# Second-layer attention: the first pass in blocks of 64 queries by 192 keys on quarters and halves of TensorE, and the next group's k and q fetched block by block

## Chip, core and metric

The kernel runs on one core of a Trainium2 chip. The metric is device time in microseconds (us), the median of some runs. Engines are named as in the profile: PE (TensorE, matrix multiply; PEld its weight loads), DVE (VectorE), ACT (ScalarE), POOL (GpSimd) and SP (SyncE, which issues most DMAs). DVE and ACT read PE's results from PSUM, which has eight banks of 512 float32 values in each of 128 partitions.

## The reference

Two layers follow each other on `x` of shape 2 x 2048 x 256. Each computes `xn = layernorm(x)`, a self-attention `s` of `xn`, a gate `g = silu(ffn(xn))`, and `x + s * g`. The change touches the second layer's attention, which is local:

```
qkv = x @ w_qkv + b_qkv          # 16 heads of 16 values
mask = 0 where |query - key| <= 64, else -inf
scores = q @ k.T * 0.25 + mask
attn = softmax(scores)
out = (attn @ v) @ w_out + b_out
```

So a query sees at most 129 keys, those up to 64 places before and after it. Everything is float32. The first layer's attention sees all keys, and uses the same functions with `local` false.

## The kernel before

**Layout.** `attention()` works by items: batch `b` (2), group `g` of four heads (4), and block `n` of 512 queries (4), 32 items in all. Of an item, q and k of the four heads lie in the four quarters of 32 partitions (`hp[j]`): 16 values of a head, then a row that holds minus the maximum in q and ones in k, so that the product `k.T q` comes out with the maximum already taken off. `qs` and `ks` hold two groups each, of all 2048 positions; k has 64 zeros (`PAD`) at either end. `fetch` (L581) reads the group after the next from DRAM (`qd`) into the tile of the group that is done, in two halves of 1024 positions, one after the group's second block and one after its fourth: four DMAs a group, on SP.

**A step.** In the second layer an item has two steps (`U = 2`), each of 256 queries, and 64 steps make the loop. `scores` (L596) issues two things side by side for a step:

- the second pass (`sk`, L611): scores with keys in partitions and queries along the row, for the step's 256 queries. Per head a bank of 512 columns, from three matmuls of 256, 128 and 128 columns. ACT takes the exponential out of PSUM (L683), POOL sets what lies outside the band to zero (L688).
- the first pass (`sq`, L653), five steps ahead (`LEAD + U`): scores with queries in partitions. Per head and tile of 128 queries one matmul against 256 keys (at the sequence's ends 192, by `reach`), in which the band lies. DVE adds a mask and takes the row's maximum in one instruction (`seen`, L674).

The four heads are in different partitions of q and k, so their matmuls use different quarters of PE's rows. When both passes are issued together (`apart`), the second pass of heads 0 and 1 stands beside the first pass of heads 2 and 3, and then the other way round. The list of matmuls is sorted by a number `when` that is written by hand: how far into the step a matmul belongs, in units of one matmul of 256 columns.

Two steps later `weigh` (L733) sums the values with the exponentials as weights (`acc`, L747): per head 128, 256 and 128 columns, the four heads in four groups of 32 columns of PE. ACT copies the result (`av`, L752).

**Maxima.** Once an item (so every second step), three steps ahead of its second pass, `place_max` (L714) turns the maxima with PE (`pmx`, L720); ACT changes the sign (`row`, L723) and issues the DMA that writes them into q (L726).

**After an item** a chain of DMAs on SP divides by the sums: `away` (L773, `ad`), `compact` (L782 and L783), `write` (L789), `spread` (L796, `recb`) and `divide` (L802, on POOL and DVE in turn). After the last group of a batch, `project` (L835, `pr`) multiplies by the output weights, and the result goes to `x` and out.

**Buffers.** PSUM's banks: `pmax` has two tiles of two banks, for `sq`; `pexp` has four of one bank, which sk, acc, pmx and pr take in turn. When an instruction of PE waits for a buffer, all later ones of PE wait with it.

The order on each engine is that of the program, settled when the program is built by a planner that knows the tiles' uses; instructions under `pin` keep their place.

Of the kernel before, what the change touches and what calls it, by code (L numbers as in the profile page):

```python
# [10 lines left out]
F32 = mybir.dt.float32  # L11
I32 = mybir.dt.int32
AF = mybir.ActivationFunctionType
ALU = mybir.AluOpType
# [3 lines left out]
P = 128  # L18
# [4 lines left out]
NG = 4  # L23
HP = 32
HV = HD + 1
TB = 512
# [11 lines left out]
def two_layers(ctx: ExitStack, tc: tile.TileContext, a, out):  # L38
# [445 lines left out]
    def attention(A, scale, local, final, start=None, projected=False):  # L484
# [18 lines left out]
        with ExitStack() as st:  # L503
# [43 lines left out]

            mp, op = pool("mp", 2), pool("op", 1)
            hp = [slice(j * HP, (j + 1) * HP) for j in range(NG)]
            ep = None if local else pool("ep", 8)  # L550


            pmax, pm = pool("pmax", 2, space=PSUM), pool("pexp", 4, space=PSUM)
            if local:

                mask = mp.tile([P, 2 * P], F32, name="mask", bufs=1)
                nc.vector.memset(mask, 0.0)
                nc.gpsimd.affine_select(
                    out=mask, in_=mask, compare_op=ALU.is_ge, fill=MASKED, base=0,
                    pattern=[[1, 2 * P]], channel_multiplier=-1,  # L560
                )
                nc.gpsimd.affine_select(
                    out=mask, in_=mask, compare_op=ALU.is_ge, fill=MASKED, base=P,
                    pattern=[[-1, 2 * P]], channel_multiplier=1,
                )

                efirst = xn[1].rearrange("p c t -> p (c t)").rearrange("p (i s c f) -> p i s c f", i=4, c=2, f=P)
                elast = op.tile([P, 2, 4, 2, P], F32, name="elast")
                ecount = [0]

                def exponentials():

                    r = ecount[0] % 6
                    ecount[0] += 1
                    return efirst[:, r] if r < 4 else elast[:, r - 4]
# [2 lines left out]
                b, g, n = items[i]  # L578
                return qs[(b * NG + g) % 2], ks[(b * NG + g) % 2], vs[b]

            def fetch(bg, lo=0, hi=T):  # L581

                if bg >= B * NG:
                    return
                b, g = divmod(bg, NG)
                k0, k1 = max(lo - PAD, 0), (T if hi == T else hi - PAD)
                for i, t in ((1, qs[bg % 2]), (0, ks[bg % 2])):
                    to, s = (slice(lo, hi), slice(lo, hi)) if i else (slice(PAD + k0, PAD + k1), slice(k0, k1))
                    nc.sync.dma_start(out=t[:, to], in_=qd[i, b, bass.ts(g, NG), :, s].rearrange("h w t -> (h w) t"))

# [5 lines left out]
            def scores(second, first, es):  # L596
# [7 lines left out]
                if second:  # L604
                    i, u = second
                    b, g, n = items[i]
                    q, k, _ = tiles(i)
                    if local:

                        qt = n * TT + 2 * u  # L610
                        segs = [  # L611
                            (P, 3 * P, bass.ts(qt + 1, P), bass.ds(qt * P, 2 * P)),
                            (0, P, bass.ts(qt, P), bass.ts(qt, P)),
                            (3 * P, 4 * P, bass.ts(qt + 2, P), bass.ts(qt + 1, P)),
                        ]
                    else:
                        segs = [(0, TB, bass.ts(u, P), bass.ts(n, TB))]
                    if local:
                        slots = [exponentials() for _ in range(2)]
                        for j in range(NG):  # L620
                            es[j] = slots[j // 2][:, 2 * (j % 2) : 2 * (j % 2) + 2].rearrange("p s c f -> p (s c f)")
                    else:
                        for j in range(NG):
                            es[j] = ep.tile([P, TB], F32, name="e", tag="e")
                    spare = None
                    for j in range(NG):
                        if not apart and j >= 2:
                            if spare is None:
                                spare = pmax.tile([P, 2, TB], F32, name="sk2", tag="sq")
                            t = spare[:, j - 2]  # L630
                        else:
                            t = pm.tile([P, TB], F32, name="sk", tag="m")
                        when = 2 * (j // 2) if apart else 0
                        for lo, hi, ks_, qs_ in segs:
                            pieces.append((when, t[:, lo:hi], k[hp[j], ks_], q[hp[j], qs_]))
                            when += 2 * (hi - lo) / TB
                        tasks.append((es[j], t))
                pairs = []
                if first:
                    i1, u1 = first  # L640
                    b1, g1, n1 = items[i1]
                    q1, k1, _ = tiles(i1)
                    if i1 not in part:
                        part[i1] = (
                            mp.tile([P, NG, TT], F32, name="mx", tag="mx"),
                            None if local else mp.tile([P, NG, TT, NB], F32, name="part", tag="part"),
                        )
                    mx, pt = part[i1]
                    for pair in ((2, 3), (0, 1)):
                        sq = pmax.tile([P, 2, TB], F32, name="sq", tag="sq")  # L650
                        pairs.append((pair, sq))
                        for d, j in enumerate(pair):
                            when = (2, 2, 0, 0)[j] if apart else 0  # L653
                            if local:
                                for t in range(2):
                                    qt, lo, hi = reach(n1, u1, t)
                                    pieces.append((
                                        when + t, sq[:, d, t * 2 * P + lo : t * 2 * P + hi],
                                        q1[hp[j], bass.ts(qt, P)], k1[hp[j], qt * P + lo : qt * P + hi],
                                    ))  # L660
                            else:
                                t, kb = divmod(u1, NB)
                                pieces.append((
                                    when, sq[:, d], q1[hp[j], bass.ds(n1 * TB + t * P, P)], k1[hp[j], bass.ts(kb, TB)]
                                ))
                for _, o, lhs, rhs in sorted(pieces, key=lambda x_: x_[0]):
                    nc.tensor.matmul(o, lhs, rhs, start=True, stop=True)  # L667
                for pair, sq in pairs:
                    if local:
                        for d, j in enumerate(pair):  # L670
                            for t in range(2):
                                qt, lo, hi = reach(n1, u1, t)
                                seen = mp.tile([P, 2 * P], F32, name="seen", tag="seen")
                                nc.vector.tensor_tensor_reduce(  # L674
                                    seen[:, lo:hi], sq[:, d, t * 2 * P + lo : t * 2 * P + hi], mask[:, lo:hi],
                                    1.0, LOWEST, ALU.add, ALU.max, mx[:, j, 2 * u1 + t : 2 * u1 + t + 1],
                                )
                    else:
                        nc.vector.tensor_reduce(pt[:, pair[0] : pair[1] + 1, t, kb], sq, AX.X, ALU.max)  # L679
# [4 lines left out]
                if second and local:  # L684
                    for e in slots[::-1]:

                        for c, sign in ((0, -1), (1, 1)):
# [1 line left out]
                                out=e[:, :, c, :], in_=e[:, :, c, :], compare_op=ALU.is_ge, fill=0.0, base=0,  # L689
                                pattern=[[0, 4], [sign, P]], channel_multiplier=-sign,  # L690
                            )

            def reach(n, u, t):

                qt = n * TT + 2 * u + t
                return qt, (PAD if qt == 0 else 0), (2 * P - PAD if qt == NT - 1 else 2 * P)

            pin = tc.keep_in_program_order

# [159 lines left out]
            for i, (b, g, n) in enumerate(items):  # L859
                if local:  # L860
                    at(i * U - LEAD, place_max, i)
                else:
                    at(i * U - LEAD, turn_max, i)
                    at(i * U - LEAD + 3, fetch_max, i)
                end = (i + 1) * U

                hops = (0, 1, 3, 4, 5, 7, 8) if local else (0, 2, 4, 5, 7, 11, 13)
                steps = (away, compact, invert, write, spread, divide)
                if i >= len(items) - (NB if local else 1):

                    hops, steps = (0, 1, 2), (last_there, last_back)
                    if not local:
                        continue
                for hop, f in zip(hops, steps):
                    at(end + DEL + hop, f, i)
                if g == NG - 1:
                    for oc in range(NC):
                        at(end + DEL + hops[-1] + oc, project, i, oc)
                if local and n == NB // 2 - 1:
                    at(end, fetch, b * NG + g + 2, 0, T // 2)  # L880
                if n == NB - 1:
                    at(end, fetch, b * NG + g + 2, T // 2 if local else 0)
            if start:
                at(0, start)
            if not local:
# [304 lines left out]
```

## Time and profile before

| what | us |
|---|---|
| median of three runs (2533.64 to 2539.33) | 2537.28 |
| the profiled execution | 2538.34 |
| its span, first to last instruction | 2536.6 |
| PE busy in it | 2513.1 |
| DVE busy | 1686.2 |
| ACT busy | 1620.8 |
| POOL busy | 876.6 |
| local attention: first first-pass matmuls | from 2248.2 |
| its first sum (acc) | 2298.8 |
| its last sum | 2519.3 |

The profile times every instruction of one execution. A row of groups gives line, engine, operation, shapes and count, then the busy time and the mean of one in ns, then the idle time before them and what ended it. A float32 matmul shows as two records, since PE makes two passes over its columns; records of different quarters overlap, so that PE's busy time isn't a measure of its work. A timeline gives start, length, engine, line and operation, with like neighbours merged. The chain lists what ended last, step by step back from the end; SPq and ACTq in it are DMAs being issued by these engines.

### The profile page before, as it was taken

To read this page: it belongs to the slowest core of one execution; us is meant where nothing else is said; L and a number is where in the kernel's file an instruction comes from. 1 tells how busy PE (TensorE), PEld (TensorE's weight loads), DVE (VectorE), ACT (ScalarE), POOL (GpSimd) and SP (SyncE) were. 2 spreads that over 40 slices of the span, in tenths; PEclk is the share of its full clock that TensorE was granted. 3 is DMA by queue.
4 is the path that set the end of the run, shared out by engine and by line. 5 is a ranking of instruction groups with operands and counts; after the bars stand their busy time and mean duration, and the time that the engine had idled before them with its cause. 6 is when DMAs were issued, how large, how long until landed. Compare 5 with 4: busy or idle time off the path is not lost.

```text
span 2536.6 us, 47898 instructions
## 1 busy us (share of the span) xinstructions
PE 2513.1 (99%) x18896; PEld 1060.6 (42%) x18896; DVE 1686.2 (66%) x2747; ACT 1620.8 (64%) x3187; POOL 876.6 (35%) x827
## 2 busy tenths in 40 slices
PE   8999999999999999999999999999999999999999
PEld 6444444444333333333333333333333334457766
DVE  4143333157888888888777788788888765238986
ACT  5400000126888888888888888888888886227755
POOL 0000000102444444444444444444444420016887
PEclk9999999999999999999999999999999999999999
DMA  6131111230001001001001001001000002133552
GB/s 243 50 84 51 52 51 39 82 118 14 14 14 43 16 12 44 16 12 44 16 12 43 10 18 44 12 17 43 15 14 10 14 14 63 49 133 108 163 167 81
DMA packets 146353, 129.83 MB, mean 51 GB/s; under 512 B 93456, under 2 KB 97936, under 8 KB 143568
## 3 DMA queue, kind: packets, MB, share of 16 engines
q1 hardware_dynamic: 144256, 125.46, 16.5%
q8 instruction: 148, 2.42, 0.4%
q10 hardware_dynamic: 1872, 1.31, 0.2%
q14 instruction: 77, 0.63, 0.1%
HBM read 80.50 MB, written 45.97 MB: 50 GB/s over the span
## 4 chain that ended last, share of the span: by engine, by line
PE 79%; DMA 1%; ACT 0%; POOL 0%; DVE 0%; issue 0%; ACTq 0%; SPq 0%; POOLq 0%; DVEq 0%
PE sk L667 25%; PE acc L747 22%; PE sq L667 19%; PE pp L477 5%; PE pr L835 2%; PE pp L532 2%; PE po L1027 1%; PE pt L1023 1%; PE po L1035 1%; PE xb L113 0%; PE xb L138 0%; DMA k<-qd 0%; PE of L827 0%; DMA q<-qd 0%; POOL xn L688 0%
## 5 line engine op out<-in xcount | busy, mean ns | idle before, releaser
L679 DVE TENSOR_REDUCE part<-sq 128x2 f32<-128x1024 f32 x1024 | 1207.3, 1221 | 294.3 <-PE sq L667 284.7
L683 ACT ACTIVATE e<-sk 128x512 f32<-128x512 f32 x2048 | 1058.3, 603 | 217.2 <-PE sq L667 197.7
L667 PE MATMUL sk<-q,k 32*128 32x512 f32 (+2 forms) x5632 | 1135.8, 533 | 1.2 <-ACT xn L683 1.0
L667 PE MATMUL sq<-k,q 32*128 32x512 f32 (+2 forms) x5120 | 1129.1, 569 | 0.5 <-DVE part L679 0.5
L761 POOL TENSOR_TENSOR av<-av,more 128x512 f32<-128x512 f32 x459 | 581.4, 1267 | 936.3 <-ACT more L760 931.1
L667 PEld LDWEIGHTS sk<-q,k 32*128 32x128 f32 x5632 | 522.0, 184 | 604.1 <-ACT e L683 512.5
L747 PE MATMUL acc<-e,v 128*32 128x512 f32 x4096 | 546.7, 605 | 0.0
L667 PEld LDWEIGHTS sq<-k,q 32*128 32x128 f32 x5120 | 402.3, 183 | 22.3 <-DVE part L679 13.2
L760 ACT COPY more<-acc 128x512 f32<-128x512 f32 x459 | 268.7, 585 | 1.2 <-PE acc L747 1.0
L747 PEld LDWEIGHTS acc<-e,v 128*32 128x32 f32 x4096 | 81.8, 108 | 388.2 <-ACT e L683 367.8
L461 ACT ACTIVATE gt<-po 128x512 f32<-128x512 f32 x16 | 8.8, 594 | 321.1 <-PE po L457 321.1
L674 DVE CUSTOM_DVE_ANT_0 seen<-sq,mask 128x256 f32<-128x256 f32 (+1 forms) x512 | 176.2, 410 | 53.6 <-PE sq L667 49.2
L467 POOL TENSOR_TENSOR x<-x,up 128x512 f32<-128x512 f32 x16 | 23.1, 1461 | 450.1 <-DVE up L464 277.5
L448 DVE TENSOR_TENSOR xs<-we,px 128x512 f32<-128x512 f32 x64 | 43.9, 686 | 136.2 <-PE px L440 130.3
L688 POOL TENSOR_SCALAR_AFFINE_SELECT xn<-xn 128x512 f32<-128x512 f32 x172 | 106.2, 652 | 77.4 <-ACT xn L683 75.7
L440 PE MATMUL px<-xn,FV 128*128 128x512 f32 x256 | 121.2, 595 | 0.0
L444 PE MATMUL py<-cum,FW 128*128 128x512 f32 x256 | 120.5, 593 | 0.6 <-DVE cum L412 0.6
L424 PE MATMUL po<-pr,UO 128*128 128x512 f32 x256 | 119.0, 592 | 0.0
L683 ACT ACTIVATE xn<-sk 128x512 f32<-128x512 f32 x172 | 89.8, 602 | 41.1 <-PE sk L667 17.9
L450 DVE TENSOR_TENSOR pr<-xs,py 128x512 f32<-128x512 f32 x64 | 44.0, 687 | 64.8 <-PE py L444 64.6
L424 PEld LDWEIGHTS po<-pr,UO 128*128 128x128 f32 x256 | 48.6, 190 | 61.2 <-issue 61.0
L444 PEld LDWEIGHTS py<-cum,FW 128*128 128x128 f32 x256 | 48.4, 190 | 61.5 <-issue 59.8
(195 smaller groups left out, 1604.0 us busy)
## 6 DMA issues: line engine op xcount, KB each, us to landing
we<-wd SPq DMA_DIRECT2D x128, 128.0 KB
ad<-av SPq DMA_DIRECT2D x59, 256.0 KB
qd<-sb SPq DMA_DIRECT2D x48, 256.0 KB
k<-qd SPq DMA_DIRECT2D x10, 1024.0 KB
q<-qd SPq DMA_DIRECT2D x10, 1024.0 KB
xn<-ad SPq DMA_DIRECT2D x59, 128.0 KB
recb<-rd SPq DMA_DIRECT2D x59, 128.0 KB
q<-qd SPq DMA_DIRECT2D x12, 512.0 KB
```

The lines of the kernel that those rows point to most:

```text
L424: nc.tensor.matmul(po[oc], UO[:, ch, bass.ts(oc, P)], pr, start=(ch == 0), stop=False)
L440: nc.tensor.matmul(px, FV[:, c, bass.ts(ch, P)], xn[b][:, c, cols], start=(c == 0), stop=(c == NC - 1))
L444: nc.tensor.matmul(py, FW[:, c, bass.ts(ch, P)], cum[:, c, :], start=(c == 0), stop=(c == NC - 1))
L477: nc.tensor.matmul(ps, w[:, c, bass.ts(hf, P)], xn[b][:, c, bass.ts(n, TB)], start=(c == 0), stop=(c == NC - 1))
L667: nc.tensor.matmul(o, lhs, rhs, start=True, stop=True)
L674: nc.vector.tensor_tensor_reduce(seen[:, lo:hi], sq[:, d, t * 2 * P + lo : t * 2 * P + hi], mask[:, lo:hi], 1.0, LOWEST, ALU.add, ALU.max, ...
L679: nc.vector.tensor_reduce(pt[:, pair[0] : pair[1] + 1, t, kb], sq, AX.X, ALU.max)
L683: nc.scalar.activation(e, t, AF.Exp, scale=scale)
L688: nc.gpsimd.affine_select(out=e[:, :, c, :], in_=e[:, :, c, :], compare_op=ALU.is_ge, fill=0.0, base=0, pattern=[[0, 4], [sign, P]], chann ...
L747: nc.tensor.matmul(acc[hp[j], o : o + hi - lo], vs[b][:, kt, vcols(g, j)], es[j][:, lo:hi], start=(r == 0), stop=(r == len(parts) - 1), sk ...
L760: nc.scalar.copy(more, acc)
L761: nc.gpsimd.tensor_tensor(avs[i], avs[i], more, ALU.add)
```

## The change

The first pass handles 64 queries instead of 128 at a time. They need 64 + 2 x 64 = 192 keys (`RC`). Two such halves of a tile of 128 queries go to the two halves of PE's columns, and so to the two halves of the 128 partitions of PSUM: for each head and tile, two matmuls of 64 columns of weights against 192 columns instead of one of 128 against 256. DVE then takes the maximum over 192 columns. The mask is laid out anew for it, in three forms (inside, first and last tile): the old one, now called `reach`, is built as before, and six copies and two memsets on DVE make the new one. Zeros that stand before the first and after the last key are now multiplied and masked, where they were left out before.

The second pass keeps its columns, but its weights (128 keys) go in two halves of 64 as well, with six matmuls a head for three. In the list of matmuls a pair's first pass counts 0.75 a tile in place of 1, and in the second half of a step the second pass's heads 2 and 3 start at 1.5.

`fetch` is called after every block of 512 instead of after two: first k's block, then, one step later, q's. That makes eight DMAs a group of 256 KB each, for four of 480 to 544 KB.

```diff
+            halves = [slice(sub * P // 2, (sub + 1) * P // 2) for sub in range(2)]
+            RC = P + 2 * PAD // 2
...
+                mask = mp.tile([P, 3, RC], F32, name="mask", bufs=1)
+                for m in range(3):
+                    for sub, p in enumerate(halves):
+                        nc.vector.tensor_copy(mask[p, m, :], reach[p, sub * PAD : sub * PAD + RC])
+                nc.vector.memset(mask[halves[0], 1, :PAD], MASKED)
+                nc.vector.memset(mask[halves[1], 2, RC - PAD :], MASKED)
...
-            def fetch(bg, lo=0, hi=T):
+            def fetch(bg, lo=0, hi=T, which=(1, 0)):
...
-                for i, t in ((1, qs[bg % 2]), (0, ks[bg % 2])):
+                for i in which:
+                    t = (ks, qs)[i][bg % 2]
...
                         segs = [
-                            (P, 3 * P, bass.ts(qt + 1, P), bass.ds(qt * P, 2 * P)),
-                            (0, P, bass.ts(qt, P), bass.ts(qt, P)),
-                            (3 * P, 4 * P, bass.ts(qt + 2, P), bass.ts(qt + 1, P)),
+                            (sub, lo, hi, bass.ds((qt + kt) * P + sub * PAD, PAD), bass.ds(q0, hi - lo))
+                            for kt, lo, hi, q0 in (
+                                (1, P, 3 * P, qt * P), (0, 0, P, qt * P), (2, 3 * P, 4 * P, (qt + 1) * P)
+                            )
+                            for sub in range(2)
                         ]
...
-                        when = 2 * (j // 2) if apart else 0
-                        for lo, hi, ks_, qs_ in segs:
-                            pieces.append((when, t[:, lo:hi], k[hp[j], ks_], q[hp[j], qs_]))
-                            when += 2 * (hi - lo) / TB
+                        when = [1.5 * (j // 2) if apart and local else 2 * (j // 2) if apart else 0] * 2
+                        for sub, lo, hi, ks_, qs_ in segs:
+                            o = t[:, lo:hi] if sub is None else t[halves[sub], lo:hi]
+                            pieces.append((when[sub or 0], o, k[hp[j], ks_], q[hp[j], qs_]))
+                            when[sub or 0] += 2 * (hi - lo) / TB
...
                                 for t in range(2):
-                                    qt, lo, hi = reach(n1, u1, t)
-                                    pieces.append((
-                                        when + t, sq[:, d, t * 2 * P + lo : t * 2 * P + hi],
-                                        q1[hp[j], bass.ts(qt, P)], k1[hp[j], qt * P + lo : qt * P + hi],
-                                    ))
+                                    for sub in range(2):
+                                        q0 = (n1 * TT + 2 * u1 + t) * P + sub * PAD
+                                        pieces.append((
+                                            when + t * RC / (2 * P), sq[halves[sub], d, bass.ts(t, RC)],
+                                            q1[hp[j], bass.ds(q0, PAD)], k1[hp[j], bass.ds(q0, RC)],
+                                        ))
...
-                                seen = mp.tile([P, 2 * P], F32, name="seen", tag="seen")
+                                qt = n1 * TT + 2 * u1 + t
+                                seen = mp.tile([P, RC], F32, name="seen", tag="seen")
                                 nc.vector.tensor_tensor_reduce(
-                                    seen[:, lo:hi], sq[:, d, t * 2 * P + lo : t * 2 * P + hi], mask[:, lo:hi],
+                                    seen, sq[:, d, bass.ts(t, RC)], mask[:, (qt == 0) + 2 * (qt == NT - 1), :],
...
-                if local and n == NB // 2 - 1:
-                    at(end, fetch, b * NG + g + 2, 0, T // 2)
-                if n == NB - 1:
-                    at(end, fetch, b * NG + g + 2, T // 2 if local else 0)
+                if local:
+
+                    for hop, which in enumerate((0, 1)):
+                        at(end + hop, fetch, b * NG + g + 2, n * TB, (n + 1) * TB, (which,))
+                elif n == NB - 1:
+                    at(end, fetch, b * NG + g + 2)
```

## The prediction

> **What bounds the kernel now.** I read the page's chain first: all of the end is TensorE (PE), and the stage that the diff touches, the second layer's attention, is its last 310 us. DMA carries 1%.
>
> ```profile
> span 2536.6 us, 47898 instructions
> PE 79%; DMA 1%; ACT 0%; POOL 0%; DVE 0%; issue 0%; ACTq 0%; SPq 0%; POOLq 0%; DVEq 0%
> ```
>
> Then the windows of this stage: columns are PE, weight load, DVE, ACT, POOL, clock, DMA share, GB/s. In the plain stretch four engines are nearly full: DVE 90%, POOL 86%, ACT 74%. Nothing can be sped up far before the next one binds. The second line is the stretch with output projections (`pr`), where PE alone is full. The clock is 1.00, so no gain or loss comes from it.
>
> ```profile
> 2340.00:2360.00 20.00, 19.83 (x401) 15.86 (x399) 17.90 (x103) 14.73 (x34) 17.11 (x27) 1.00 0.48 147
> 2420.00:2440.00 20.00, 19.96 (x282) 12.87 (x278) 15.06 (x74) 9.96 (x23) 16.33 (x22) 1.00 0.49 163
> ```
>
> Third, groups by form in this stage, for prices. A matmul here is two records (two fp32 passes).
>
> ```profile
> L674 DVE CUSTOM_DVE_ANT_0 seen<-sq,mask 128x256 f32<-128x256 f32 x412 | 148.9, 418 | 17.7 <-PE sq L667 13.4 <-PE sk L667 4.2 <-issue 0.2
> L667 PE MATMUL sq<-k,q 32*128 32x256 f32 x824 | 111.1, 392 | 0.0
> L674 DVE CUSTOM_DVE_ANT_0 seen<-sq,mask 128x192 f32<-128x192 f32 x60 | 21.1, 352 | 2.5 <-PE sq L667 2.4
> L667 PE MATMUL sq<-k,q 32*128 32x192 f32 x120 | 16.6, 339 | 0.0
> ```
>
> Last, the timelines of PE and its weight loads over one step (256 queries, four heads). It has a score block (sk and sq side by side) from 2345.19, the sums acc from 2347.30, and, every second step, the turn of the maxima pmx; the next score block begins at 2348.51.
>
> ```profile
> 2345.19 0.48 PE L667 MATMUL sk<-q,k 32*128 32x256 f32 x2
> 2345.20 0.48 PE L667 MATMUL sq<-k,q 32*128 32x256 f32 x2
> ...
> 2345.51 0.38 PE L667 MATMUL sk<-q,k 32*128 32x256 f32 x2
> 2345.52 0.38 PE L667 MATMUL sq<-k,q 32*128 32x256 f32 x2
> 2345.72 0.27 PE L667 MATMUL sk<-q,k 32*128 32x128 f32 x2
> ...
> 2347.30 1.08 PE L747 MATMUL acc<-xn,v 128*32 128x128 f32 x24
> 2348.31 0.28 PE L720 MATMUL pmx<-ident,mx 128*16 128x128 f32 x1
> 2348.51 0.62 PE L667 MATMUL sk<-q,k 32*128 32x256 f32 x2
> 2348.66 0.48 PE L667 MATMUL sq<-k,q 32*128 32x256 f32 x2
> ```
>
> A pass over 256 columns takes 2345.72 - 2345.51 = 0.213 us, and all four row quarters start within 0.02 us. So a block has 8 passes per quarter, 1.71 us; its first weight load is exposed (0.32 - 0.213 = 0.107), and about 0.19 us of drain follow: 2.0 us. With `pr` it takes 1.95 to 2.04 (2412.47 to 2414.42, 2417.45 to 2419.49). In plain steps it takes 2.11, because DVE is late: its eight `seen` at 0.345 us fill 2.76 us, and the second half's sq waits for them. Starts of acc give 3.26 us a step (2298.85 to 2409.55, 34 steps), 4.98 with `pr` (8 steps, to 2449.36), then 14 plain ones to 2496.33.
>
> A second loop hides under this. The sk tiles, acc and pmx share four PSUM buffers in turn. With pmx between, the second sk of a block takes the buffer of the fourth exponential before:
>
> ```profile
> 2346.48 2.12 ACT L683 ACTIVATE elast<-sk 128x512 f32<-128x512 f32 x4 [0.71 <-POOL xn L688]
> 2348.49 0.38 ACT L752 COPY av<-acc 128x256 f32<-128x256 f32 x1
> 2348.74 0.26 ACT L723 ACTIVATE row<-pmx 16x128 f32<-16x128 f32 x1
> ```
>
> The four exponentials end at 2348.60; the sq that queue behind this second sk start at 2348.66. That is why sk and sq lie 0.15 us apart there and 0.01 us at 2345.19.
>
> **The change part by part.**
>
> *First pass, 64 queries by 192 keys.* Per head and 128 queries, one matmul 128x256 becomes two of 64x192, in the two column halves of PE. If the halves run together, a quarter needs 1.5 instead of 2 units of 0.427 us: -0.213 a block. The first load is of 64 columns: I take half of 0.107, -0.053 (0 to 0.1). The block: 0.05 + 3.5 x 0.427 + 0.19 = 1.74 us. `seen` is 192 wide everywhere: the rows show 418 against 352 ns, so the interval falls from 0.345 to 0.279 us, DVE from 2.76 to 2.23 us a step, and its wait before the second half goes.
>
> *Second pass in halves too.* sk has 48 weight loads and matmuls instead of 24, the same columns. The trace has no eight tiles (four quarters by two halves) at once. The nearest rows are the four quarters above and acc's four column groups: 24 records of acc in 1.08 us. The Trainium skill ("TensorE: Matmul & The Clock Gate", "Wait — 56ns, not 53.3ns?") says against this that start-to-start never drops below about 25 ns; 80 records at 25 ns would be 2.0 us, the block as long as now, and the sum only DVE's relief and the fetches, about -4. Here two sk and two sq start within 0.02 us, so I keep 1.74, and -12.6 below. From both sides: 1.74 with full overlap, 0.05 + 7 x 0.427 + 0.19 = 3.23 with none; I take the lower, by those two rows, and carry the other as a rival.
>
> *What then binds.* PE alone: 1.74 + 1.00 (acc) + 0.10 (pmx in half of the steps) = 2.84. But the buffers now bind. The first exponential starts 1.29 us after its block (2345.19 to 2346.48), 1.24 after the change; three intervals of 0.49 and 0.60 for the last make 3.31, and 0.05 to PE: 3.36 from a block to the second sk of the next block with pmx (now 2348.65 - 2345.19 = 3.46). The other step of the pair is PE's, 1.74 + 1.00 = 2.74 (now 2345.19 - 2342.15 = 3.04). A pair: 6.10 instead of 6.50, 0.20 a step. Other engines fit: ACT has 5.6 a pair (8 x 0.49, 2 x 0.38, row 0.26, DMA issue 0.55, waits), POOL 0.86 x 6.5 = 5.6. 48 plain steps: -9.6. With `pr`, acc must wait for the first exponential (1.24 + 0.60 + 0.05 = 1.89 against 2.0): 8 x 0.12 = -1.0. Five first-pass blocks ahead of the loop (16 records in 1.07 us): 0.2 each, -0.9 in all.
>
> *The fetches.* Four DMAs a group become eight, 256 KB each: 24 more issues on SP at about 0.55 us. SP then has some 4.0 of 6.1 us an item, and is in order: its `recb` waits (41.1 us in 23 waits) stand in front of fetches, which have seven to eight steps (over 20 us) until they are read. So no cost, and if the cover is gone, up to 2 us a late block. A gain is visible: the row DMA on ACT uses a semaphore that a fetch of half a row holds, and ACT's exponentials queue behind it.
>
> ```profile
> 2383.52 5.28 DMA k<-qd
> 2388.88 0.53 ACTq L726
> 2463.97 4.83 DMA q<-qd
> 2468.87 0.54 ACTq L726
> ```
>
> The steps there take 3.67 and 4.45 us (acc 2386.58 to 2390.25, 2465.81 to 2470.26): 1.4 us over. 256 KB lands in 3.55 (`ad` in the same chain) instead of about 5, so the wait should shrink below its slack: -1.1 (from -1.4 to +2, should the smaller ones meet more often).
>
> *Mask.* Two memsets and six copies on DVE, beside the mask's selects at 2132 us; the first `seen` is at 2249. The nearest row, its memset, is 272 ns: 2.2 us, hidden in a stretch where DVE is busy 11 of 20 us; 0 taken, +2 if it delays norms.
>
> Sum: -9.6 - 1.0 - 0.9 - 1.1 = -12.6. The profiled execution took 2538.3 (span 2536.6 and 1.7 around it), 1.1 above the median: 2525.7 on that run, about **2525** against 2537.3.
>
> **Rivals.** *Buffers don't bind* (their turn may fall differently in the new order): PE's 2.84 + 0.03 a step, 48 x 0.39 = 18.7, `pr` 8 x 0.26 = 2.1, with the rest -22.8: 2514.5. Against it: the 0.15 us gap above. Chance 0.10.
>
> *Less comes through:* the block stays at 1.9 to 2.0 because eight tiles are fed less evenly, or ACT, 92% full, delays its pairs. DVE's relief, the fetches and a part of the rest remain, -3 to -7: 2530 to 2534. Chance 0.22.
>
> *Halves take turns* (slower). If a row quarter feeds only one column half at a time, the block is 3.23 and a step 4.33 us: 48 x 1.07 = 51, `pr` 8 x 1.23 = 10, ahead of and behind the loop about 5: +66, 2603. It decides as soon as the block exceeds 2.2 us on the average, the halves together over 1.3 times one. For it: no such mix in the trace. Against: both kinds of split run together here. Chance 0.10.
>
> *Fetches do not help:* more DMAs meet the row DMA or delay SP; 2 to 8 us back: 2527 to 2533, or in the worst case past the time before. Chance 0.08.
>
> **Numbers.** Forecast 0.50, rivals as above. About 0.2% (5 us) is what a measurement of this kernel tells from no change; below 2532.2 is faster. Slower: 0.10 for the halves, 0.02 for fetches: 0.12. Same: 0.08, from the weak ends of two rivals. Faster 0.80. The range is 2515 to 2535.
>
> **What would show it.** Right: sq rows 32*64 with 192 columns; `seen` 352 ns; block 1.75 to 1.9 us; plain steps near 3.05, alternating about 2.75 and 3.35; DVE below 80%, ACT and POOL over 90%; no L726 with a fetch in the chain. Wrong: blocks over 2.2 us with halves starting a pass apart; or equal steps of 2.85 (buffers free); or new waits of ACT or SP for `k<-qd`.

## The result, and the profile after

The changed kernel takes 2565.44 us (median of 4 runs, 2557.77 to 2570.71), the kernel before 2537.49 (4 runs, 2533.64 to 2539.33). The ratio is 1.011, 95% interval 1.008 to 1.014: slower by 28 us. The prediction said 2525, with a range of 2515 to 2535. The profiled execution after took 2557.77 with a span of 2556.0, so the traces below hold 19.4 us of the loss.

The page after: its first line, the shares of the chain by engine, and the row of one DMA queue (packets, MB, share of the 16 DMA engines).

```profile
span 2556.0 us, 53087 instructions
...
q8 instruction: 168, 2.75, 0.5%
...
PE 78%; issue 1%; ACT 1%; DVE 1%; DMA 1%; POOL 0%; ACTq 0%; SPq 0%; DVEq 0%
```

The same queue on the page before:

```profile
q8 instruction: 148, 2.42, 0.4%
```

"issue" has come into the chain: PE waits for nothing that the profile names. And q8, which carries instructions, has 20 packets more. The first section of the two pages gives PE 18,896 matmuls and as many weight loads before, 21,456 and as many after: 5,120 instructions more, 256 for each packet of 16 KB. The prediction uses neither row.

The windows of the stage (PE, weight load, DVE, ACT, POOL, clock, DMA share, GB/s); the second is again in the stretch with `pr`:

```profile
2340.00:2360.00 20.00, 17.37 (x536) 12.77 (x535) 13.33 (x87) 12.70 (x29) 13.96 (x22) 0.91 0.57 152
2440.00:2460.00 20.00, 19.94 (x449) 12.73 (x450) 13.33 (x74) 10.24 (x24) 16.69 (x22) 1.00 0.62 172
```

No engine is full in the plain stretch any more, PE is busy in 17.37 of 20 us, and the clock is 0.91 (more of this below). With `pr`, PE is as full as before. Two of the groups by form:

```profile
L690 DVE CUSTOM_DVE_ANT_0 seen<-sq,mask 128x192 f32<-128x192 f32 x512 | 148.1, 353 | 92.7 <-PE sq L683 83.4 <-PE sk L683 8.9
L683 PE MATMUL sq<-k,q 32*64 32x192 f32 x2048 | 115.6, 341 | 2.5 <-issue 2.5
```

The change does what it says: 32*64 tiles of 192 columns, and `seen` at 353 ns. The timeline of PE over a step that nothing disturbs:

```profile
2329.83 1.08 PE L758 MATMUL acc<-xn,v 128*32 128x128 f32 x24
2330.84 0.28 PE L731 MATMUL pmx<-ident,mx 128*16 128x128 f32 x1
2331.05 0.59 PE L683 MATMUL sk<-q,k 32*64 32x256 f32 x4
2331.22 0.40 PE L683 MATMUL sq<-k,q 32*64 32x192 f32 x4
...
2332.70 0.33 PE L683 MATMUL sk<-q,k 32*64 32x128 f32 x4
2333.09 1.08 PE L758 MATMUL acc<-xn,v 128*32 128x128 f32 x24
```

From acc to acc 3.26 us, and 2.95 in the step ahead of it (acc at 2326.88): 6.21 a pair against 6.50. Two halves of four quarters run together. But ten microseconds earlier the same timeline has this:

```profile
2318.98 0.33 PE L683 MATMUL sk<-q,k 32*64 32x128 f32 x4
2319.39 0.27 PE L758 MATMUL acc<-xn,v 128*32 128x128 f32 x1
2322.17 1.93 PE L758 MATMUL acc<-xn,v 128*32 128x128 f32 x23 [2.51 <-issue]
2324.04 0.38 PE L731 MATMUL pmx<-ident,mx 128*16 128x128 f32 x1
```

PE has done one of acc's 24 records and stops for 2.5 us in the middle of a group that has all of its data, then needs 1.93 us for the rest instead of about 1. The chain of waits has such pieces all through the stage, and one of the other kind, where ACT's row DMA is late:

```profile
2319.66 2.51 issue
...
2343.91 1.79 issue
...
2367.23 2.58 issue
...
2482.79 4.50 DMA k<-qd
2487.37 0.53 ACTq L737
```

The stalls have a pattern. Counting all of PE's instructions (matmuls, weight loads and its waits for semaphores) from the start of the trace, the stops of over half a microsecond between 2290 and 2520 us that end in nothing named all come at an index of 193 modulo 256: at the border of a block of 256 instructions. The trace has as many packets of q8 as such borders (148 before, 168 after). Between 2296 and 2408 us one packet follows each border, and PE goes on past the next border only 1.1 us or more after that packet has landed. So one block is on its way at a time. At 2315.83 PE crossed a border; the packet was not moved until 2319.98. The DMA queues in between, as 40 slices of the busy share (in tenths) and the data queue's row:

```profile
DMA  4459957499333499746954899999997842101006
...
q1 hardware_dynamic: 553, 0.77, 67.5%
```

SP had issued k at 2313.69, q at 2314.97 and `ad` at 2316.07, 800 KB together, and the 16 DMA engines were busy with data until about 0.7 us before the packet (a slice is 0.1 us; only the last eight are low). PE used up its 256 instructions at 2319.4 and stood until 2322.17.

The Trainium skill ("Runtime: NRT & Kernel Launch", "Instruction fetch mechanics") says that an engine's instructions are refilled in blocks of 16 KiB, 256 instructions, by DMA, and that crossing a block's border is "mostly hidden". The size agrees with the trace; that it is hidden holds for the kernel before and not for this one. Read from the traces between 2296 and 2408 us, all times in us; a stall is counted from the last start before the border to the first one after it:

| kernel | PE instructions in a plain step | blocks | a block lasts (mean) | border to refill, mean (range) | landing to first use (range) | stalls over 0.5 at a border |
|---|---|---|---|---|---|---|
| before | 128 | 17 | 6.39 | 1.20 (0.04 to 2.76) | 2.38 to 5.56 | none |
| after | 208 | 25 | 4.58 | 2.05 (1.06 to 4.33) | 1.13 to 2.59 | 9, of 14.6 in all |

Before, a block lands 0.7 us or more ahead of need: the stalled kernels show 1.1 to 1.7 us from landing to use as the least. After, a block would last 3.82 us in undisturbed steps (3.105 x 256 / 208), and a refill takes longer than that on the mean: 2.05 of wait, about 1 for the packet, and 1.1 or more until use.

The stalls have a second price, the clock. Two windows of the changed kernel, the stall at 2319.66 with what lies around it, and the 3.4 us behind it:

```profile
2318.80:2322.20 3.40, 0.81 (x37) 0.43 (x21) 2.10 (x15) 1.91 (x4) 2.85 (x5) 1.00 0.28 92
2322.20:2325.60 3.40, 3.40 (x56) 2.52 (x63) 0.00 (x0) 0.54 (x2) 0.06 (x1) 0.50 0.68 165
```

PE gets half of its clock for 3.4 us, which is why the rest of acc took 1.93 us. The same happens at 2346.1, 2370.0 and 2489.4 (the last behind a late row); the kernel before has no such stretch in its attention. And PE stops outside of the borders too, behind each of three late row DMAs, longest here:

```profile
2488.74 1.31 PE L758 MATMUL acc<-xn,v 128*32 128x128 f32 x24 [3.25 <-ACT elast L699]
```

A rough account of the profiled execution from 2290 to 2520 us: 12 stalls at borders, 17.3 us; three stops behind late rows, 5.5 (0.74, 1.52 and 3.25); four stretches at half the clock, at most 1.7 each, 6.8. That is some 30 us lost against some 10 gained (the shorter undisturbed steps, and a first acc that came 2.7 us earlier in this execution), for 19.4 in all. It is an estimate: the parts may overlap, and an idle moment may hide another wait.

### The profile page after: what moved, and what is told of

It reads as the page before. It is cut to its first block, busy times and chain, and to the rows that moved or that the text cites. A ratio compares the mean times of both kernels' runs of the same rounds, so it can differ in the third digit from the quotient of the medians.

```text
span 2556.0 us, 53087 instructions
## 1 busy us (share of the span) xinstructions
PE 2511.3 (98%) x21456; PEld 1051.5 (41%) x21456; DVE 1660.9 (65%) x2755; ACT 1621.9 (63%) x3187; POOL 876.3 (34%) x827
## 3 DMA queue, kind: packets, MB, share of 16 engines
q8 instruction: 168, 2.75, 0.5%
## 4 chain that ended last, share of the span: by engine, by line
PE 78%; issue 1%; ACT 1%; DVE 1%; DMA 1%; POOL 0%; ACTq 0%; SPq 0%; DVEq 0%
PE sk L683 24%; PE acc L758 22%; PE sq L683 19%; PE pp L477 4%; PE pr L846 2%; PE pp L532 2%; PE po L1040 1%; PE pt L1036 1%; PE po L1048 1%; ACT xn L699 0%; PE xb L138 0%; ACT elast L699 0%; PE xb L113 0%; DVE seen L690 0%; DMA ad<-av 0%
## 5 line engine op out<-in xcount | busy, mean ns | idle before, releaser
L683 PE MATMUL sq<-k,q 32*128 32x512 f32 (+1 forms) x6144 | 1118.8, 524 | 3.0 <-issue 2.5
L683 PEld LDWEIGHTS sk<-q,k 32*128 32x128 f32 (+1 forms) x7168 | 508.5, 162 | 611.1 <-ACT e L699 512.6
L683 PEld LDWEIGHTS sq<-k,q 32*128 32x128 f32 (+1 forms) x6144 | 387.6, 167 | 26.6 <-DVE part L695 13.2
L690 DVE CUSTOM_DVE_ANT_0 seen<-sq,mask 128x192 f32<-128x192 f32 x512 | 148.1, 353 | 92.7 <-PE sq L683 83.4
```

What stands on the lines that cost most here:

```text
L690: nc.vector.tensor_tensor_reduce(seen, sq[:, d, bass.ts(t, RC)], mask[:, (qt == 0) + 2 * (qt == NT - 1), :], 1.0, LOWEST, ALU.add, ALU.max ...
```

## The experiments

Time from acc to acc in each stretch of the second layer, from the traces (us):

| kernel | 34 plain steps | 8 with `pr` | 14 plain steps |
|---|---|---|---|
| before | 110.77 | 39.81 | 46.97 |
| after | 129.35 | 39.23 | 51.35 |
| e1, passes only | 125.95 | 40.61 | 47.37 |
| e2, fetches only | 123.90 | 42.67 | 46.47 |
| e4, before with acc in pieces | 129.86 | 40.52 | 48.74 |
| e5, after without fetches | 109.80 | 39.22 | 46.61 |
| e8, after with acc in pieces | 159.55 | 43.15 | 67.05 |
| e9, e2 with fetches behind rd and ad | 111.24 | 39.82 | 46.48 |
| e10, after with the same | 133.00 | 39.99 | 52.89 |

**e1: the new passes with the old fetches.**

```diff
-                if local:
-                    for hop, which in enumerate((0, 1)):
-                        at(end + hop, fetch, b * NG + g + 2, n * TB, (n + 1) * TB, (which,))
+                if local and n == NB // 2 - 1:
+                    at(end, fetch, b * NG + g + 2, 0, T // 2)
```

> Both passes in column halves as in the changed kernel, fetches in half rows as before. Theory 1 (PE runs dry of instructions: after every 256 weight loads and matmuls it stands still until the next 16 KB of them has landed): stalls at the same places, 104 pairs a step as in the change, so 2550 to 2562 us. Theory 2 (the eight tiles on PE are slow): the same time, but longer score blocks instead of stalls every 256 records. Theory 3 (the smaller, more frequent fetches cause the loss, by holding semaphores or crowding the queues): about 2525 us, as predicted.

Measured: 2553.46 us against 2537.04 (the kernel before on the same chip), ratio 1.0064 (1.0039 to 1.0089). The weight loads of its trace between 2280 and 2500 us, with the idle time ahead of them and what ended it (before, the three rows have 5.2, 0.3 and 5.1 of issue):

```profile
L683 PEld LDWEIGHTS sk<-q,k 32*64 32x64 f32 x2640 | 84.6, 131 | 25.1 <-issue 15.1 <-ACT xn L699 4.9 <-ACT elast L699 1.6
L683 PEld LDWEIGHTS sq<-k,q 32*64 32x64 f32 x1792 | 65.0, 131 | 6.6 <-issue 5.3 <-DVE mx L690 0.8
L758 PEld LDWEIGHTS acc<-xn,v 128*32 128x32 f32 x856 | 25.5, 109 | 21.1 <-issue 12.6 <-POOL elast L704 1.9 <-POOL xn L704 1.5
```

So the passes alone make it slower, with stalls at the same borders: 7 over 0.5 us between 2296 and 2408, 15.7 us in all.

**e2: the old passes with fetches a block at a time.** The reverse of e1's edit, on the kernel before.

> The passes as before, k and q fetched a block at a time as in the change. Theory 1: instruction blocks last over 6 us here, so no stall of PE every 256 records; only the row DMA of ACT can meet a fetch more or less often than before: 2533 to 2546 us. Theory 2: the same. Theory 3: most of the loss is here, 2555 us or more.

Measured: 2549.48 us, ratio 1.0052 (1.0035 to 1.007). No stall at a border; here it is ACT. SP's timeline, and then the chain:

```profile
2356.50 0.54 SPq L590 DMA_DIRECT2D k<-qd  x1
2357.14 0.37 SPq L590 DMA_DIRECT2D q<-qd  x1
2357.56 0.58 SPq L790 DMA_DIRECT2D rd<-dn  x1
```

```profile
2357.46 4.86 issue
2362.32 0.55 ACTq L727
...
2362.97 0.61 ACT elast L684
```

`row` is ready at 2357.46. Ahead of its DMA, ACT waits for two semaphores. One is that of the small `rd<-dn` (8 KB), which was issued just behind nearly 512 KB of k and q; its last part landed at 2362.25, ACT issues at 2362.32, and its exponentials queue behind. The other is that of `q<-qd`, and it had landed only at 2361.60. Four of the five late rows wait for both, with `rd` last by 0.2 to 0.65 us. Row DMAs are late by 1.91 us in all in the kernel before, by 12.99 here. PE stops behind them, and here too its clock is 0.50 after two of these stops, for 6.8 us each from 2362.0 and 2423.4.

**e3: halves in the first pass only**, the second with whole key tiles as before, old fetches.

```diff
-                            (sub, lo, hi, bass.ds((qt + kt) * P + sub * PAD, PAD), bass.ds(q0, hi - lo))
+                            (None, lo, hi, bass.ts(qt + kt, P), bass.ds(q0, hi - lo))
```

> First pass in halves (64 queries by 192 keys), second pass with 128 keys of weights as before, fetches as before. 80 pairs of weight load and matmul a step instead of 104 (before: 64). Theory 1: an instruction block lasts 256/160 steps, some 4.9 us, and most refills come in time: 2524 to 2532 us, unless PE drains between weights of 128 and of 64 columns (then blocks of over 2.2 us and 2540 or more). Theory 2 (tiles of half the columns are slow): a part of the loss, 2545 us or more. Theory 3: 2525 to 2530.

Measured: 2779.33 us, ratio 1.0949 (1.0928 to 1.0971). PE's timeline:

```profile
2396.32 1.22 PE L682 MATMUL sk<-q,k 32*128 32x256 f32 x4
2397.48 1.56 PE L682 MATMUL sq<-k,q 32*64 32x192 f32 x16
2398.96 1.25 PE L682 MATMUL sk<-q,k 32*128 32x128 f32 x12
2400.14 0.92 PE L682 MATMUL sq<-k,q 32*64 32x192 f32 x8
```

The two shapes take turns: sk, then sq, then sk, a block of 7 us (2396.32 to the acc at 2403.29), and the clock from 2320 to 2400 is 0.50. A part of the 7 us is the clock: two blocks that the loop's start runs at 1.00 take 7.6 us together (2289.67 to the pmx at 2297.24), 3.8 each, still nearly twice the 2.0 of the kernel before. The Trainium skill ("TensorEngine Tiling (Array Packing)", "Key Properties") says that a change of tiling mode drains the engine; the two kinds of tile behave so here. My rival of halves that take turns is thus real, but for unlike shapes. Splitting the second pass too avoids this price, with 48 loads and matmuls in place of 24; their number is what costs next.

**e4: the kernel before, with only acc cut into pieces of 64 columns**: as many PE instructions a step as the change has (208), the old passes, columns and fetches.

```diff
+                    parts = tuple(
+                        (o + s_, lo + s_, lo + s_ + 64, kt) for o, lo, hi, kt in parts for s_ in range(0, hi - lo, 64)
+                    )
```

> The kernel before with one edit: the sums (acc) are made from matmuls of 64 columns of queries instead of 128 or 256. The same sums and the same columns through PE, no column halves in the scores, no new fetches, but 104 pairs a step, exactly as many as in the change. Theory 1: PE stands still every 256 records just as in the changed kernel, 2550 to 2575 us. Theories 2 and 3: acc takes 0 to 0.3 us longer a step, 2537 to 2555 us, without gaps every 256 records.

Measured: 2555.40 us, ratio 1.0071 (1.005 to 1.0093). A step of PE's timeline, with the cut in the middle of sq this time, and the queue's row on the page:

```profile
2307.50 0.48 PE L667 MATMUL sq<-k,q 32*128 32x256 f32 x2 [2.23 <-issue]
```

```profile
q8 instruction: 168, 2.75, 0.5%
```

Nothing of the change is in this kernel but its number of instructions, and it loses 18 us, with stalls at the same borders (9, of 14.7 us between 2296 and 2408).

**e5: the changed kernel without fetches** after the first two groups.

```diff
-                    for hop, which in enumerate((0, 1)):
+                    for hop, which in enumerate(()):
```

> The changed kernel without its fetches of k and q after the first two groups of each half; it leaves out that data and computes with the groups that are there. Question: why do blocks of TensorE's instructions come late. If the small DMAs that bring them queue behind the fetches' 256 KB, the stalls at every 256th record go, no row DMA of ACT is held either, and only the gain of the clean steps is left: 2525 to 2532 us. If a block of 256 instructions simply cannot be fetched faster than about once in 3.8 us, the stalls stay and only the held row DMAs go: 2548 to 2558 us. In between, 2532 to 2548: the fetches are one of several sources of the wait.

Measured: 2539.65 us (12 runs) against 2541.75 (17 runs), ratio 0.9991 (0.998 to 1.0002). Windows from 2320 to 2400 us, first of the changed kernel, then of this one:

```profile
2320.00:2400.00 80.00, 69.64 (x2156) 52.59 (x2156) 53.78 (x347) 50.31 (x114) 58.16 (x89) 0.94 0.53 138
```

```profile
2320.00:2400.00 80.00, 77.12 (x2580) 60.93 (x2584) 63.65 (x411) 59.43 (x137) 68.90 (x105) 1.00 0.31 89
```

The DMA share falls from 0.53 to 0.31, the refill starts 1.29 us after a border instead of 2.05 (never later than 2.60), and the long stalls are gone: 4 over 0.5 us, 2.9 in all. It is my "in between" case. Fetches on the DMA engines make the refills late; but even without them a block of 256 is used up about as fast as the next one comes, and of the 7 us that undisturbed steps would give (48 x 0.145) only 1.3 are left (110.77 + 46.97 less 109.80 + 46.61). Here a block is used 1.1 to 1.95 us after it has landed, at all borders but one between 2296 and 2408, close to the 1.1 to 1.7 of the stalls. So I estimate that an order of the fetches that met no refill at all would still leave this change within 0.2% of the kernel before, by the interval's lower end.

**e6: the kernel before, with the row sent by SP; e7: the same with e2's fetches.** I wanted to free ACT from its own row DMA.

```diff
-                pin((nc.scalar if local else nc.sync).dma_start(
+                pin(nc.sync.dma_start(
```

> The kernel before with the row of maxima sent by SP instead of ACT. Theory: ACT stands for 1.9 us in all behind row DMAs whose semaphore is held by a fetch, and pays about 0.55 us of issue an item. If the row on SP is sent in time: 2533 to 2537 us. Rival: SP is in order too, its waits for recb and for semaphores stand in front of the row, the score blocks that need the row come late: 2540 to 2555 us.

> The kernel before with fetches of k and q a block at a time (as in e2, 2549.5 us), and with the row of maxima sent by SP. Theory: the loss of e2 is ACT standing behind its own row DMA. Then the time falls to 2534 to 2540 us. Rival: the row itself, not ACT, is what is late, since the semaphore is held whoever sends it, or SP's own queue now delays it; then TensorE's score blocks wait for the row and the time stays at 2545 to 2560 us.

Measured: e6 2551.29 us (1.0035, 1.0021 to 1.0048), e7 2554.63 (1.0053, 1.0037 to 1.007), both against 2541.75. The group of sk in e6, then in e7:

```profile
L667 PE MATMUL sk<-q,k 32*128 32x512 f32 (+2 forms) x5632 | 1139.5, 534 | 8.4 <-DMA q<-row 7.1
```

```profile
L668 PE MATMUL sk<-q,k 32*128 32x512 f32 (+2 forms) x5632 | 1137.4, 533 | 14.1 <-DMA q<-row 13.5
```

The rival holds for e6: now it is the row itself that is late, in SP's order, and PE waits for it. Since SP costs that much alone, e7 says little about e2's cause; e9 had to decide.

**e8: the changed kernel with acc in pieces as in e4**, 288 PE instructions a step.

> The changed kernel with the second layer's acc matmuls cut into pieces of 64 columns: 288 instead of 208 TensorE instructions a plain step, the same columns. If the supply of instructions is the limit, with a block of 256 needed every 2.7 us and arriving not much faster than once in about 4 us on the mean, a plain step becomes 4 to 5 us and the time 2590 to 2640 us. If the stalls of the change come from something else that happens a fixed number of times, the cut costs no more than it cost the kernel before (18 us), and the time is 2565 to 2585 us.

Measured: 2618.65 us, ratio 1.0307 (1.0293 to 1.0321). The page's chain, and one acc in the timeline:

```profile
PE 78%; issue 3%; DVE 0%; ACT 0%; DMA 0%; POOL 0%; ACTq 0%; DVEq 0%; POOLq 0%
```

```profile
2336.75 1.10 PE L761 MATMUL acc<-xn,v 128*32 128x64 f32 x64
2337.78 0.28 PE L731 MATMUL pmx<-ident,mx 128*16 128x128 f32 x1
```

Uncut by a border, 64 records take 1.10 us where 24 took 1.08: the pieces themselves are free. But 159.55 / 34 is 4.69 us a step, and from 2302 to 2408 us the 26 blocks last 4.18 us on the mean, with a stall at nearly every border (24 over 0.5 us, 32.7 in all); the shortest lasts 3.36. This is the supply's own rate, 256 instructions in 4.2 us beside these fetches, and 4.18 x 288 / 256 = 4.70 is the step. The first theory holds, at its number.

**e9: e2 with the fetches of an item behind its rd and ad in SP's queue; e10: the changed kernel with the same; e11: the kernel before, its fetches of half a row there.**

```diff
-                        at(end + hop, fetch, b * NG + g + 2, n * TB, (n + 1) * TB, (which,))
+                        at(end + 2, fetch, b * NG + g + 2, n * TB, (n + 1) * TB, (which,))
```

In `fetch`, the second layer's DMAs are also kept in this place of the order (`pin`).

> The kernel before with k and q fetched a block at a time (as in e2, 2549.5 us), but the two fetches of an item now stand in SP's queue behind that item's rd and ad instead of ahead of them; nothing else moves. Theory: e2 loses because ACT's row DMA has to wait for the small rd<-dn, which stands behind 512 KB of fetches on the DMA engines. Then the row DMA is held no more and the time is 2534 to 2541 us. Rival: it is the fetches themselves, more of them, that the row waits for, wherever they stand: 2546 to 2555 us.

> The changed kernel (2565 us) with the same reordering of its fetches behind rd and ad. Theory: only the held row DMAs go, about 8 to 12 us, and the stalls at every 256th instruction stay, because the fetches still share the DMA engines with the instruction blocks: 2550 to 2558 us. If the stalls went too, 2530 to 2540 us; if nothing is gained, 2560 us and more.

> The kernel before with its fetches of half a row placed behind rd and ad in SP's queue. A candidate for a version that is faster than both: the row DMAs of ACT are held for 1.9 us in all in the kernel before. Theory: 2534 to 2537 us, hardly to be told from no change. Rival: a fetch of 512 KB behind ad now holds the next item's dn and xn, 2540 us and more.

Measured: e9 2537.42 us (13 runs) against 2536.74 (25 runs), ratio 1.0002 (0.9993 to 1.001); e10 2571.99, 1.0133 (1.0118 to 1.0149); e11 2536.51, 1.0001 (0.9993 to 1.0009). SP's timeline in e9:

```profile
2352.77 0.58 SPq L790 DMA_DIRECT2D rd<-dn  x1
2353.40 0.79 SPq L774 DMA_DIRECT2D ad<-av  x1
2354.28 0.47 SPq L590 DMA_DIRECT2D k<-qd  x1
2355.58 0.32 SPq L590 DMA_DIRECT2D q<-qd  x1
```

`rd` goes out first, no row DMA is late any more (0.0 us in all), and the 12 us of e2 are gone with the same bytes in the same eight fetches a group. That settles e2: not the size or the number of the fetches, but their place in SP's queue, ahead of what the row waits for. The fetch of q also moves away from the row by this, so e9 does not tell `rd`'s wait from q's own.

e10 went against me. The row DMAs are late by 2.99 us instead of 8.28, yet the kernel gains nothing. A row of its weight loads between 2280 and 2500 us, which in the changed kernel has 12.1 of issue:

```profile
L683 PEld LDWEIGHTS sk<-q,k 32*64 32x64 f32 x2506 | 82.1, 136 | 28.3 <-issue 19.8 <-ACT xn L699 4.2 <-ACT elast L699 1.4
```

Between 2296 and 2408 there are 14 stalls of 19.2 us in all instead of 9 of 14.6, and up to 2520 there are five stretches at half the clock instead of four. Fetches still meet refills, now at other moments; why there are more such meetings I did not separate. So what the rows gained, the stalls took. That the losses of e1 (16.4) and e2 (12.4) add up to the change's 28 is no proof that the two costs simply add: each order of DMAs has other stalls.

No version here beats the kernel before: e5, e9 and e11 cannot be told from it.

## Why the prediction was wrong

- *What bounds the kernel.* The reading of the engines was right as far as it went. It left out a resource that no engine row shows: the supply of PE's instructions, 128 a step before, each block 0.7 us or more early.
- *Second pass in halves too* is the step that failed. I asked of the 48 loads and matmuls whether PE overlaps them (3.23 us if not) and whether it starts them fast enough (25 ns each by the Trainium skill, "TensorE: Matmul & The Clock Gate", "Wait — 56ns, not 53.3ns?", so 2.0 us), and of nothing else. Overlap was right. On the starts the trace is below that floor of 25 ns: the 80 records of an undisturbed block start within 1.59 us (2327.89 to 2329.48), 20 ns each, and e8's acc has 64 in 1.10. But 2.0 would have been nearer to the block than my 1.74. What the step put at nothing is that 80 more instructions a step (48 for this pass, 32 for the first) have to be delivered: the two passes alone cost +16.4 us (e1), and e4 shows +18 for as many instructions, with none of the change in it.
- *First pass.* `seen` came out at 353 ns (352 predicted), and DVE fell to 13.33 of 20 us, in part because PE stops (about 15.9 of 20 in e5, where it hardly does). The block was mis-sized: measured as I had done, from its first sk to acc, it takes 1.94 and 2.04 us in undisturbed steps (2327.89 to 2329.83, 2331.05 to 2333.09) against 1.74. That is no less than the 1.95 to 2.04 of the kernel before where DVE was not late; against the 2.11 of its plain steps only DVE's delay is gone. What spaces its passes is not settled.
- *What then binds.* The pair of steps alternates as predicted, 2.95 and 3.26 against 2.75 and 3.35: 6.21 against 6.10. That would have been -7.0 instead of -9.6 for 48 plain steps; late refills, late rows and the lower clock behind them turned it into +23.0 (+18.6 and +4.4 in the table).
- *With `pr`:* predicted -1.0, measured -0.6. PE's instructions are sparser there, and no border has a stall from 2425 to 2465.
- *Blocks ahead of the loop:* predicted -0.9. The first acc comes 2.7 us earlier, but over the kernels of the table its time varies from 2295.7 to 2301.8, so I claim none of it.
- *The fetches:* predicted -1.1, with +2 as the worst; alone they cost +12.4 (e2). I had found the right mechanism, a row DMA held by another transfer's semaphore, and then sized it by the fetch's own duration. A held row waits for every DMA whose semaphore it needs, the small `rd` included, and the finer fetches stand ahead of that one in every item. Of the changed kernel's three late rows one waits longest for `rd`, one for `ad` and one for the k fetch itself (2482.79).
- *Rivals.* "Less comes through" describes the undisturbed steps. "Halves take turns" gave the slower side by a mechanism that e3 shows only for mixed shapes. None of them had instructions in it. Of the signs of being right, the alternating undisturbed steps, `seen` and the 32*64 rows came true, the block did not; of the signs of failure, a wait of ACT for `k<-qd` came (2482.79).

## What to carry to other kernels

Before splitting matmuls, count PE's instructions per microsecond in the stage, weight loads included, and compare that with the packets of the instruction queue: here 256 in 6.4 us were safe, and 256 in 3.8 us were not while data DMAs ran. A stall marked "issue" in the middle of a group with all its data, at equal distances in PE's instructions, is the supply. In an in-order queue, put small transfers that others wait for ahead of large ones that nobody needs soon. And look at the granted clock behind every stop of PE: the stop may not be all that it costs.

## What was new about the hardware

- PE's instructions come one block of 256 at a time. In e8, where PE always waits for them, a block took 3.36 us at the least and 4.18 on the mean. Where a refill landed in time, a border shows no gap (before: none over 0.5 us at 17 borders).
- The clock fell to 0.50 four times in the changed kernel. In the 3.4 us ahead of each fall PE was busy in 0.81, 1.53, 0.82 and 0.66 us of 3.40. The starts of these stretches lie 23.9, 23.9 and 119.5 us apart, multiples of 3.41, so they seem to fall on a fixed grid. That would explain e4, whose stalls are as long: its clock fell at 2308.6, where the 3.4 us ahead of it held 1.18 us of PE, and not at 2370.0 and 2390.5, where they held 1.48 and 1.82, since those stalls lie across two places of the grid. Where the limit lies is not settled: 1.53 was too little in the changed kernel, and 1.48 enough in e4.
- Tiles of 32x128 and 32x64 took turns (e3), at full clock (3.8 us a block) and at half (7.0); those of sk and sq run together when both are 32x64.
